# Shifted-window attention and a Fourier layer on one core: two groups transformed back in other rows, attention banks in strict turn, values fetched by ScalarE in three rows of eight, queries ahead of the late exponential

## The chip, the core and the metric

The kernel runs on one core of a Trainium2 chip. The metric is the device time of one execution in microseconds (us); the kernel before is measured in three runs and given by their median. All profile times come from one further, profiled execution.

A core has four engines that compute, and each works through its own queue in order: TensorE (PE; its weight loads are shown as PEld), ScalarE (ACT), VectorE (DVE) and GpSimd (POOL). SyncE (SP) issues most of the DMAs. [...]TensorE writes to PSUM, eight banks of 2 KB for each of 128 partitions.

## The reference, cut to what matters

Input: 32 images of 56x56 pixels and 128 channels, float32. Two layers, each added to its input:

```python
# layer 0: group norm (32 groups), then attention in shifted 7x7 windows, 4 heads of 32
x = x + attention(_gn(x), rpb_table, w_qkv, w_proj, b_proj)
#   q, k, v = win @ w_qkv.T;  softmax(q k^T * 32**-0.5 + bias + mask) v;  @ w_proj.T + b_proj
# layer 1: group norm, then a cosine transform along each axis, cut to 32 modes and mixed
h = _forward_fourier(_gn(x), w0, w1)
#   xy = idct(einsum('bixy,ioy->boxy', dct(x, axis=-1)[..., :32], w0)); xx: the same along the other axis
x = x + (relu(h @ W1 + b1) @ W2 + b2)
```

All of it is computed in float32.

## The kernel before, in words

**Rows.** The work is cut into rows: one row is 7 lines of one image, that is 8 windows. An image has 8 rows, and the 32 images have 256. The main loop counts cycles; in cycle r the products, scores and softmax of row r are made, the value product with the softmax belongs to row r-3, and so does the projection at the cycle's end. Below, "row 7" stands for a cycle whose number leaves 7 when divided by 8, "row 12" and greater numbers for single cycles. Cycles 0 to 10 (`first_rows`) carry attention alone. From cycle 11 on (`CONV_BEGIN`) each cycle also carries a share of the second layer of the image before: an image's own count `c` begins at 0 in its row 3 and goes to 15, so two images are in it at a time. After cycle 258 the second layer alone is left.

**Order.** The loop is inside `tc.manual_schedule` for TensorE, ScalarE, VectorE and GpSimd: on each of them instructions stand in the order in which the Python code emits them. SyncE's order is made by the scheduler of the Tile layer, which also sets every semaphore and gives buffers to tiles.

**A row's steps on the engines.**

- TensorE: q and k (`attn_qk`, L422, by `halved`, L113), ff_in (L113, from `xf`), the values (L549: softmax, turned, times v), a cosine transform (L705) in rows 3 to 5, the scores (L480), transforms back (`modes_back`, L792), the value product v (`attn_v`, L458), mixing of modes (`mix`, L753), ff_out (L113, from `hid`) and the projection (L594).
- ScalarE: copies of q (L435) and k (L445) out of PSUM, the squares for the second norm (`attn_squares`, L631), ReLU (`hid`, L837), half of the attention output (`oT`, L581), the copies of v (L465) and z (L761), the scaling of modes (L728), the exponential (`attn_exp`, L505), once an image the scaled weights `wn` (L414).
- VectorE: sums for the softmax (`sm`, L510) and its inverse, copies of projected rows (`x`, L602) and results (L880), the other half of oT in three instructions (L579: 147, 28 and 21 elements), the copies of the scores with bias (L488), their maximum (L498), transposes of modes (`turn_modes`, L721), adding the transform back to `xf` (`fetch_back`, L810), the transpose of the softmax (L534) and, in row 7, the chain of the first norm (`image_norm`, L382 to L411).
- GpSimd: subtracts the maximum (L499), divides by the sum (L524), adds biases (L127, L842), raises to the power -0.5 (L406).

**Banks.** Attention has four banks of PSUM under one tag (`pa`); the allocator gives a tile whichever bank its own model says comes free first. The second layer has the other four (`pc`). In `attn_values` the two banks are taken in reverse, so that half u = 0, which ScalarE reads, has the second one.

**Where things stand.** `halves_first`, `eighths`, `quarters`, `last_fetch`, `columns_turn`, `behind_max` and `halves_last` are emitted one after the other in each cycle (L1235 to L1260). The exponential of a row is emitted in `halves_last`, the copy of the next row's q in the next cycle's `halves_first`. `back_groups` (L922) says when the transforms back are made, four groups a direction (16, 16, 16 and 8 lines): at c = 5 and 6 along one axis, at c = 7 and 8 (rows 2 and 3) along the other. `load_back` issues their loads (zT) a cycle ahead. `FF_AT` (L42) places ff_in and ff_out at c = 8, 9, 10, 12, 13, 14, 15. `next_tokens` (L954) loads two rows ahead into the buffer `xr` which the squares used as scratch.

Of the kernel before, what the change touches and what calls it, by code (L numbers as in the profile page):

```python
# [1 line left out]

# [45 lines left out]
def swin_fourier_kernel(  # L48
# [32 lines left out]

    def attn_bank():
        return bank("pa", 4)
# [338 lines left out]
    def attn_qk(im, i):  # L422

        def product(part):
            p = attn_bank()
            w = im.w[:, part * C : (part + 1) * C]
            halved(p[:, :RT].rearrange("p (j t) -> p j t", t=WT), w, im.xw[i])
            if i == 0:
                halved(p[:, RT : RT + 1], w, im.mean)
            return p  # L430

        pq = product(0)
        if i == 0:
            nc.scalar.mul(im.bias[:, 0:1], pq[:, RT : RT + 1], QS)
        nc.scalar.activation(  # L435
            q_sb[:, :RT], pq[:, :RT], AF.Identity, bias=im.bias[:, 0:1], scale=QS
        )
        pk = product(1)
        if i == 0:
            for u in range(2):  # L440
                nc.scalar.mul(
                    im.bias[:, 3 + u : 4 + u], pk[:, RT : RT + 1], heads[:, u : u + 1]
                )
        for u in range(2):
            nc.scalar.activation(  # L445
                k_sb[:, u],
                pk[:, :RT].rearrange("p (w j) -> p w j", j=WT),
                AF.Identity,
                bias=im.bias[:, 3 + u : 4 + u],
                scale=heads[:, u : u + 1],  # L450
            )
# [85 lines left out]
    def attn_values(im, i, r):  # L537
# [3 lines left out]
        po = [attn_bank(), attn_bank()][::-1]  # L541
# [21 lines left out]
        for u in range(2):  # L563
            src = po[u][:, :HALF].rearrange("p (r f x) -> p r f x", r=WS, f=NP)
            n = NP - u
            dst = bass.AP(
                oTr.tensor,
                oTr[:, :, SS + u * WS :].offset,
                [oTr.ap[0], [S, WS], [2 * WS, n], [1, WS]],
            )  # L570
            parts = [(dst, src[:, :, :n])]
            if u:
                parts += [
                    (oTr[:, :, S - WS + SS :], src[:, :, n, : WS - SS]),
                    (oTr[:, :, 0:SS], src[:, :, n, WS - SS :]),
                ]
            for d, f in parts:
                if u:
                    nc.vector.tensor_scalar(d, f, im.bias[:, 2:3], None, ALU.add)  # L579
                else:  # L580
                    nc.scalar.activation(d, f, AF.Identity, bias=im.bias[:, 2:3])  # L581
# [44 lines left out]
    def attn_squares(im, i):  # L626

        n0, n1 = WS * i // 2, WS * (i + 1) // 2
        piece = x1[:, n0:n1]
        sq = im.xr.pop(i)[:, : n1 - n0]  # L630
        nc.scalar.activation(sq, piece, AF.Square, scale=valid)  # L631
        nc.vector.tensor_reduce(
            im.part[:, i % 4, 1],
            sq.rearrange("p n (g c) -> p g n c", c=4),
            axis=AX.XY,
            op=ALU.add,
        )
# [77 lines left out]
    def turn_modes(im, width, h):  # L715

        im.modes[width, h] = []
        for p in im.py.pop((width, h)):
            t = work.tile([P, 4, C], F32, tag="z", name="modes", bufs=4)
            t = t.rearrange("p k c -> p (k c)")[:, : 2 * CH * KB]  # L720
            nc.vector.transpose(t, p[:, : 2 * CH * KB])  # L721
            im.modes[width, h].append(t)
# [199 lines left out]
    def back_groups(c):  # L922

        if c in (5, 6, 7, 8):
            return [(c >= 7, (c + 1) % 2 * 2 + j) for j in range(2)]
        return []
# [37 lines left out]
    def halves_first(cycle):  # L964
# [4 lines left out]
        tokens_bias(cycle)  # L969
        if cycle == CONV_BEGIN or (cycle - 1) % NWR not in EARLY:  # L970
            divide(cycle)
# [3 lines left out]
        im, i = row(cycle)  # L975
        if im:
            attn_qk(im, i)
            if i == NWR - 2:
                wrap_rows(cycle)
        if last and cycle > CONV_BEGIN:  # L980
            attn_squares(last, j)
        next_tokens(cycle)
# [36 lines left out]
    def quarters(cycle):  # L1019
        def back():  # L1020
            for im, c in fourier(cycle):
                for j, (width, g) in enumerate(back_groups(c)):
                    modes_back(im, width, g)
                    if not (c == 8 and j):
                        fetch_back(im, width, g)
# [9 lines left out]
    def eighths(cycle):  # L1035
        im, i = row(cycle - 3)
        if im:
            attn_values(im, i, cycle - 3)
        for im, c in fourier(cycle):
            if c == 0:  # L1040
                for h in range(2):
                    transform(im, True, h)
                    turn_modes(im, True, h)
# [80 lines left out]
    EARLY = (0, 3, 4, 5, 7)  # L1124

    def halves_last(cycle):
# [11 lines left out]
        if row(cycle)[0]:  # L1138
# [18 lines left out]
    def first_rows(cycle):  # L1157
        im, i = row(cycle)
        im3, i3 = row(cycle - 3)
        if im:  # L1160
            attn_qk(im, i)
# [15 lines left out]
        if last:  # L1177
            attn_squares(last, j)
            add_sums(last, j)
# [27 lines left out]
        if cycle == CONV_BEGIN - 1:  # L1207
            attn_sums(im3, i3)
            attn_squares(im3, i3)
            attn_exp(cycle)  # L1210

    ET = mybir.EngineType
    with tc.manual_schedule(engines={ET.PE, ET.Activation, ET.DVE, ET.Pool}):
# [17 lines left out]
        for cycle in range(NB * NWR + CONV_BEGIN + FF_AT[-1] - NWR + 1):  # L1231
# [4 lines left out]
            if not row(cycle - 3)[0]:  # L1236
                eighths(cycle)
                columns_turn(cycle)
# [18 lines left out]
            columns_turn(cycle)  # L1257
# [65 lines left out]
```

## Time and profile before

| what | us |
|---|---|
| runs of the kernel before: median (lowest, highest) of 3 | 3269.87 (3268.61, 3271.36) |
| profiled execution, its own time | 3275.91 |
| its span, first to last instruction | 3274.1 |
| TensorE busy | 3147.8 |
| VectorE, GpSimd, ScalarE busy | 2637.3, 2340.5, 2099.2 |
| span of rows 24 to 247 (282.6 to 3036.9) | 2754.3 |
| one image in it, 28 of them | 98.4 |

How to read it. The page slices the span in 40 and gives the busy share of an engine in each slice as a digit; busy time of TensorE holds stretches in which its pipeline refills, so it is a bound and not a measure of its pace. The view of waits adds up, for each instruction group, the time that its engine stood idle right before it, and names what ended that: "PE pa L458 <- ACT oT L581: 15.6, 29, 1.0" reads that TensorE stood 15.6 us in all, in 29 places and at most 1.0 us at once, before products of L458 into a bank `pa`, until a ScalarE instruction of L581 was done. "issue" is idle time for which no wait is seen. The view of windows gives, for a stretch, its length and each engine's busy time in it. In the timeline a line has the start, the duration, the engine, the line of code and the operands; brackets give the idle time of the engine just before.

### The profile page before, as it was taken

The page shows a single profiled execution, that of the slowest core. Times are in us where ns is not written, and L with a number is a line of the kernel's source. Part 1 is how long each engine was busy: PE and PEld are TensorE (multiplying, and loading weights), DVE is VectorE, ACT ScalarE, POOL GpSimd, SP SyncE. Part 2 cuts the span into 40 slices and gives each one's busy share as a digit, 9 for nine tenths or more (in the row PEclk, how much of TensorE's full clock was granted, in tenths as well). Part 3 has the DMA queues.
Part 4 walks back from the last instruction along what each step waited for, and adds up shares of the span by engine and source line. Part 5 has one row for each costly group of instructions (what it writes and reads, how often), then busy time and mean ns, then how long its engine had stood idle before and what let it go on. Part 6 is the DMA issues. An engine that isn't in the chain of part 4 may idle for free.

```text
span 3274.1 us, 151714 instructions
## 1 busy us (share of the span) xinstructions
PE 3147.8 (96%) x65664; PEld 2369.2 (72%) x65664; DVE 2637.3 (81%) x5066; ACT 2099.2 (64%) x3680; POOL 2340.5 (71%) x2634
## 2 busy tenths in 40 slices
PE   4689999999999999999999999999999999999999
PEld 3467777777777777777777777777777777777776
DVE  7888888888888888888888888888888888888751
ACT  3456766666666666666666666666666666666663
POOL 7767777777777777777777777777777777777741
PEclk8789999999999999999999999999999999999999
DMA  6546555655565656565656665656565656565453
GB/s 111 111 115 148 139 135 142 140 137 144 137 146 141 143 140 145 134 143 139 144 137 145 142 139 136 146 136 143 138 145 138 146 136 143 137 144 138 121 138 99
DMA packets 1173442, 448.47 MB, mean 137 GB/s; under 512 B 529483, under 2 KB 1142909, under 8 KB 1172773
## 3 DMA queue, kind: packets, MB, share of 16 engines
q1 hardware_dynamic: 1163428, 433.22, 55.9%
q8 instruction: 516, 8.45, 1.2%
q10 hardware_dynamic: 8736, 5.38, 0.7%
q14 instruction: 154, 1.25, 0.1%
q0 software_dynamic: 608, 0.17, 0.0%
HBM read 277.00 MB, written 161.48 MB: 134 GB/s over the span
## 4 chain that ended last, share of the span: by engine, by line
PE 84%; ACT 7%; DVE 2%; issue 2%; DMA 2%; SPq 2%; POOL 1%; ACTq 0%; DVEq 0%; POOLq 0%
PE pc L113 38%; PE pa L113 10%; PE pa L458 8%; PE pc L792 5%; PE pa L594 5%; PE pa L480 5%; PE pc L753 5%; PE pa L549 4%; PE pc L705 3%; ACT hid L837 2%; ACT k L445 2%; SPq L763 1%; ACT xr L631 1%; ACT z L761 1%; DMA zscr<-z 1%
## 5 line engine op out<-in xcount | busy, mean ns | idle before, releaser
L524 POOL TENSOR_TENSOR blocks<-a,rs 128x512 f32<-128x512 f32 x1506 | 1278.9, 856 | 399.2 <-DVE rs L512 253.6
L113 PE MATMUL pc<-wff,hid 128*64 128x128 f32 x12288 | 715.3, 273 | 2.4 <-ACT hid L837 1.0
L113 PE MATMUL pc<-xf,wff 128*64 128x512 f32 (+2 forms) x3584 | 714.5, 539 | 1.1 <-DVE xf L810 0.9
L113 PEld LDWEIGHTS pc<-wff,hid 128*64 128x64 f32 x12288 | 679.6, 137 | 15.0 <-ACT hid L837 5.3
L499 POOL TENSOR_TENSOR a<-a,mx 128x784 f32<-128x784 f32 x251 | 377.4, 1504 | 351.0 <-DVE mx L498 334.3
L113 PEld LDWEIGHTS pc<-xf,wff 128*64 128x64 f32 x3584 | 267.1, 136 | 368.1 <-issue 254.5
L837 ACT ACTIVATE hid<-pc,b1sb 128x512 f32<-128x512 f32 (+2 forms) x896 | 500.0, 642 | 40.7 <-PE pc L113 40.7
L113 PE MATMUL pa<-xw,wn 128*64 128x392 f32 x2048 | 397.6, 503 | 30.2 <-ACT wn L414 29.7
L465 ACT COPY v<-pa 128x512 f32<-128x512 f32 x256 | 151.7, 593 | 419.8 <-PE pa L458 417.1
L488 DVE TENSOR_TENSOR a<-pa,bm 128x392 f32<-128x392 f32 x502 | 260.3, 560 | 90.4 <-PE pa L480 72.3
L445 ACT ACTIVATE k<-pa,bqkv,heads 128x392 f32<-128x392 f32 x512 | 318.6, 674 | 15.4 <-PE pa L113 1.3
L728 ACT ACTIVATE y<-modes,rstd 128x448 f32<-128x448 f32 x256 | 276.5, 1138 | 72.8 <-DVE modes L721 64.3
L842 POOL TENSOR_TENSOR res<-res,b2sb 128x512 f32<-128x512 f32 (+1 forms) x224 | 252.3, 1126 | 87.5 <-DMA res<-scr 87.5
L534 DVE STREAM_TRANSPOSE eT<-blocks 128x1024 f32<-128x1024 f32 x256 | 313.8, 1226 | 0.9 <-POOL blocks L524 0.9
L458 PE MATMUL pa<-wn,xw 128*64 128x128 f32 x4096 | 291.3, 284 | 22.5 <-ACT oT L581 15.6
L127 POOL TENSOR_TENSOR xr<-xr,bproj 128x384 f32<-128x384 f32 (+1 forms) x256 | 292.3, 1142 | 25.7 <-DMA xr<-in_x_dram 8.9
L505 ACT ACTIVATE a<-a 128x784 f32<-128x784 f32 x251 | 215.1, 857 | 147.3 <-POOL a L499 147.1
L549 PEld LDWEIGHTS pa<-eT,v 49*32 49x32 f32 x16384 | 173.6, 106 | 159.0 <-ACT hid L837 48.7
L435 ACT ACTIVATE q<-pa,bqkv 128x392 f32<-128x392 f32 x256 | 149.2, 583 | 210.4 <-PE pa L113 208.7
L579 DVE TENSOR_SCALAR oT<-pa,bqkv 128x147 f32<-128x147 f32 (+2 forms) x768 | 171.7, 280 | 135.9 <-PE pa L549 133.2
L510 DVE TENSOR_REDUCE sm<-a 128x16 f32<-128x784 f32 x251 | 241.4, 962 | 41.1 <-ACT a L505 40.9
L458 PEld LDWEIGHTS pa<-wn,xw 128*64 128x64 f32 x4096 | 227.6, 140 | 62.0 <-ACT oT L581 29.0
(112 smaller groups left out, 5040.0 us busy)
## 6 DMA issues: line engine op xcount, KB each, us to landing
zscr<-z SPq DMA_DIRECT2D x512, 112.0 KB
xin<-in_x_dram SPq DMA_DIRECT2D x496, 112.0 KB
htok<-scr SPq DMA_DIRECT2D x256, 196.0 KB
zT<-zscr SPq DMA_DIRECT2D x192, 256.0 KB
res<-scr SPq DMA_DIRECT2D x160, 256.0 KB
out_dram<-res SPq DMA_DIRECT2D x160, 256.0 KB
scr<-x SPq DMA_DIRECT2D x256, 112.0 KB
xr<-in_x_dram SPq DMA_DIRECT2D x256, 84.0 KB
```

Of the source, the lines that this page charges most:

```text
L113: nc.tensor.matmul(dst[ps], lhsT=lhsT[:, ps], rhs=rhs, start=start, stop=stop)
L127: nc.gpsimd.tensor_tensor(piece, piece, bproj.unsqueeze(1).to_broadcast([P, n, C]), ALU.add)
L445: nc.scalar.activation(k_sb[:, u], pk[:, :RT].rearrange("p (w j) -> p w j", j=WT), AF.Identity, bias=im.bias[:, 3 + u : 4 + u], scale=head ...
L458: nc.tensor.matmul(pv[HALVES[w % 2], w // 2 * C : (w // 2 + 1) * C], lhsT=im.half[i // NP][:, t0 : t0 + JP], rhs=im.w[:, 2 * C : 3 * C], s ...
L488: nc.vector.tensor_tensor(a[:, 2 * hp : 2 * hp + 2, :, 0:WT].rearrange("p u w j -> p w u j"), ps[hp][:, :RT].rearrange("p (w u j) -> p w u ...
L499: nc.gpsimd.tensor_tensor(a3, a3, mx.unsqueeze(2).to_broadcast([P, 2 * NWR, WT]), ALU.subtract)
L524: nc.gpsimd.tensor_tensor(dst[to, k, :, :n], a3[src, :, kb * KB : kb * KB + n], rs[src].unsqueeze(2).to_broadcast([src.stop - src.start, 2 ...
L534: nc.vector.transpose(eT.rearrange("p t (k j) -> p k t j", k=2), blocks[r % 2])
L549: nc.tensor.matmul(po4[u][h * HD : (h + 1) * HD, pr], lhsT=v[ks, pr, h * HD : (h + 1) * HD], rhs=eT[ks, h * NP + pr, :WT], start=True, sto ...
L728: nc.scalar.mul(y[:, r], t.rearrange("p (n k) -> p n k", k=NM), im.rstd)
L837: nc.scalar.activation(hf[:, :n], ph[:, :n], AF.Relu, bias=b1sb[:, f : f + 1])
L842: nc.gpsimd.tensor_tensor(im.res[:, :k], im.res[:, :k], b2sb.unsqueeze(1).to_broadcast([P, k, C]), ALU.add,)
```

## The change

- `attn_bank` gives the four attention banks in strict turn, each under a tag of its own with one buffer.
- `back_groups`: the two last groups of the second direction are made at c = 10 (16 lines, row 5) and c = 12 (8 lines, row 7) instead of both at c = 8 (row 3). Their products stay behind the scores; their copies (`fetch_back`) stand behind the maximum, in `last_fetch`. `turn_modes` is split by its two banks; where c = 10, the first bank is turned ahead of the scores' copy.
- In rows 3, 6 and 7 (`VALUES_BY_ACT`) ScalarE reads both halves of oT: u = 0 first, in one instruction, then u = 1 in three. The banks are then not reversed.
- `attn_qk` is split into `attn_q` and `attn_k`. In row 7 the exponential of the row before stands between them on ScalarE; it is no more emitted at the end of row 6.
- In row 7 the squares stand behind oT on ScalarE, their sum (`sum_squares`, VectorE) behind the maximum and the copies of the moved group, ahead of the norm's chain, and the load of tokens (`next_tokens`) behind that sum.

```diff
@@ -79,8 +80,10 @@
     def bank(tag, bufs):
         return psum.tile([P, HB], F32, tag=tag, name=tag, bufs=bufs)
 
+    turns = count()
+
     def attn_bank():
-        return bank("pa", 4)
+        return bank(f"pa{next(turns) % 4}", 1)
 
     def conv_bank():
         return bank("pc", 4)
@@ -419,23 +422,26 @@
         yield
 
 
-    def attn_qk(im, i):
-
-        def product(part):
-            p = attn_bank()
-            w = im.w[:, part * C : (part + 1) * C]
-            halved(p[:, :RT].rearrange("p (j t) -> p j t", t=WT), w, im.xw[i])
-            if i == 0:
-                halved(p[:, RT : RT + 1], w, im.mean)
-            return p
-
-        pq = product(0)
+    def product_of(im, i, part):
+        p = attn_bank()
+        w = im.w[:, part * C : (part + 1) * C]
+        halved(p[:, :RT].rearrange("p (j t) -> p j t", t=WT), w, im.xw[i])
+        if i == 0:
+            halved(p[:, RT : RT + 1], w, im.mean)
+        return p
+
+    def attn_q(im, i):
+
+        pq = product_of(im, i, 0)
         if i == 0:
             nc.scalar.mul(im.bias[:, 0:1], pq[:, RT : RT + 1], QS)
         nc.scalar.activation(
             q_sb[:, :RT], pq[:, :RT], AF.Identity, bias=im.bias[:, 0:1], scale=QS
         )
-        pk = product(1)
+
+    def attn_k(im, i):
+
+        pk = product_of(im, i, 1)
         if i == 0:
             for u in range(2):
                 nc.scalar.mul(
@@ -534,11 +540,13 @@
         nc.vector.transpose(eT.rearrange("p t (k j) -> p k t j", k=2), blocks[r % 2])
         im.eT[i] = eT
 
-    def attn_values(im, i, r):
+    def attn_values(im, i, r, both=False):
 
 
         v = v_sb[r % 3]
-        po = [attn_bank(), attn_bank()][::-1]
+        po = [attn_bank(), attn_bank()]
+        if not both:
+            po.reverse()
         HALF = RT // 2
         po4 = [p[:, :HALF].rearrange("p (r n s) -> p n r s", r=WS, s=WS) for p in po]
         eT = im.eT.pop(i)
@@ -560,7 +568,7 @@
 
 
         oTr = oT[:, i % 2 * RT : (i % 2 + 1) * RT].rearrange("p (r x) -> p r x", x=S)
-        for u in range(2):
+        for u in (0, 1) if both else (1, 0):
             src = po[u][:, :HALF].rearrange("p (r f x) -> p r f x", r=WS, f=NP)
             n = NP - u
             dst = bass.AP(
@@ -575,7 +583,7 @@
                     (oTr[:, :, 0:SS], src[:, :, n, WS - SS :]),
                 ]
             for d, f in parts:
-                if u:
+                if u and not both:
                     nc.vector.tensor_scalar(d, f, im.bias[:, 2:3], None, ALU.add)
                 else:
                     nc.scalar.activation(d, f, AF.Identity, bias=im.bias[:, 2:3])
@@ -627,11 +635,14 @@
 
         n0, n1 = WS * i // 2, WS * (i + 1) // 2
         piece = x1[:, n0:n1]
-        sq = im.xr.pop(i)[:, : n1 - n0]
-        nc.scalar.activation(sq, piece, AF.Square, scale=valid)
+        im.sq = im.xr.pop(i)[:, : n1 - n0]
+        nc.scalar.activation(im.sq, piece, AF.Square, scale=valid)
+
+    def sum_squares(im, i):
+
         nc.vector.tensor_reduce(
             im.part[:, i % 4, 1],
-            sq.rearrange("p n (g c) -> p g n c", c=4),
+            im.sq.rearrange("p n (g c) -> p g n c", c=4),
             axis=AX.XY,
             op=ALU.add,
         )
@@ -712,14 +723,13 @@
             at += n
         im.py[width, h] = py
 
-    def turn_modes(im, width, h):
-
-        im.modes[width, h] = []
-        for p in im.py.pop((width, h)):
-            t = work.tile([P, 4, C], F32, tag="z", name="modes", bufs=4)
-            t = t.rearrange("p k c -> p (k c)")[:, : 2 * CH * KB]
-            nc.vector.transpose(t, p[:, : 2 * CH * KB])
-            im.modes[width, h].append(t)
+    def turn_modes(im, width, h, r):
+
+        p = im.py[width, h][r]
+        t = work.tile([P, 4, C], F32, tag="z", name="modes", bufs=4)
+        t = t.rearrange("p k c -> p (k c)")[:, : 2 * CH * KB]
+        nc.vector.transpose(t, p[:, : 2 * CH * KB])
+        im.modes.setdefault((width, h), []).append(t)
 
     def scale_modes(im, width, h, r):
 
@@ -921,9 +931,9 @@
 
     def back_groups(c):
 
-        if c in (5, 6, 7, 8):
-            return [(c >= 7, (c + 1) % 2 * 2 + j) for j in range(2)]
-        return []
+        if c in (5, 6, 7):
+            return [(c == 7, (c + 1) % 2 * 2 + j) for j in range(2)]
+        return [(True, c // 2 - 3)] if c in (10, 12) else []
 
     def load_back(cycle):
         for im, c in fourier(cycle):
@@ -967,19 +977,27 @@
         if cycle % NWR == NWR - 1:
             norm_step(cycle)
         tokens_bias(cycle)
+        im, i = row(cycle)
+        behind_short = im and i == NWR - 1
+        if behind_short:
+            attn_q(im, i)
+            attn_exp(cycle - 1)
         if cycle == CONV_BEGIN or (cycle - 1) % NWR not in EARLY:
             divide(cycle)
         if last and cycle > CONV_BEGIN:
             attn_sums(last, j)
         next_quarter(cycle)
-        im, i = row(cycle)
         if im:
-            attn_qk(im, i)
+            if not behind_short:
+                attn_q(im, i)
+            attn_k(im, i)
             if i == NWR - 2:
                 wrap_rows(cycle)
-        if last and cycle > CONV_BEGIN:
+        if last and cycle > CONV_BEGIN and not behind_short:
             attn_squares(last, j)
-        next_tokens(cycle)
+            sum_squares(last, j)
+        if not behind_short:
+            next_tokens(cycle)
         if cycle % NWR == 0:
             norm_step(cycle)
         for im, c in fourier(cycle):
@@ -1019,9 +1037,9 @@
     def quarters(cycle):
         def back():
             for im, c in fourier(cycle):
-                for j, (width, g) in enumerate(back_groups(c)):
+                for width, g in back_groups(c):
                     modes_back(im, width, g)
-                    if not (c == 8 and j):
+                    if c < 8:
                         fetch_back(im, width, g)
 
         if not has_ff(cycle):
@@ -1035,12 +1053,15 @@
     def eighths(cycle):
         im, i = row(cycle - 3)
         if im:
-            attn_values(im, i, cycle - 3)
+            attn_values(im, i, cycle - 3, cycle % NWR in VALUES_BY_ACT)
+            if cycle % NWR == NWR - 1:
+                attn_squares(*row(cycle - 4))
         for im, c in fourier(cycle):
             if c == 0:
                 for h in range(2):
                     transform(im, True, h)
-                    turn_modes(im, True, h)
+                    for r in range(2):
+                        turn_modes(im, True, h, r)
                 next(im.stats)
             if c == 1:
                 for r in range(2):
@@ -1054,13 +1075,14 @@
 
     def last_fetch(cycle):
         for im, c in fourier(cycle):
-            if c == 8:
-                fetch_back(im, *back_groups(c)[1])
-
-    def columns_turn(cycle):
+            if c > 8:
+                for width, g in back_groups(c):
+                    fetch_back(im, width, g)
+
+    def columns_turn(cycle, r):
         for im, c in fourier(cycle):
             if c in (1, 2):
-                turn_modes(im, False, c - 1)
+                turn_modes(im, False, c - 1, r)
 
     def scale_first(cycle, r):
         for im, c in fourier(cycle):
@@ -1122,6 +1144,7 @@
                 ff_out(im, FF_AT.index(c))
 
     EARLY = (0, 3, 4, 5, 7)
+    VALUES_BY_ACT = (3, 6, 7)
 
     def halves_last(cycle):
         im, i = row(cycle)
@@ -1135,7 +1158,7 @@
         next_begin(cycle)
         if cycle % NWR == NWR - 1:
             norm_step(cycle)
-        if row(cycle)[0]:
+        if row(cycle)[0] and cycle % NWR != NWR - 2:
             attn_exp(cycle)
         scale_first(cycle, 1)
         if row(cycle)[0] and cycle % NWR in EARLY:
...
@@ -1250,11 +1277,19 @@
             if not has_ff(cycle):
                 half_columns(cycle)
             eighths(cycle)
+            early = any(c == 10 for _, c in fourier(cycle))
+            if early:
+                columns_turn(cycle, 0)
             quarters(cycle)
             if row(cycle)[0]:
                 attn_max(cycle)
+            if not early:
+                columns_turn(cycle, 0)
+            columns_turn(cycle, 1)
             last_fetch(cycle)
-            columns_turn(cycle)
+            if cycle % NWR == NWR - 1 and row(cycle - 4)[0]:
+                sum_squares(*row(cycle - 4))
+                next_tokens(cycle)
             behind_max(cycle)
             load_first(cycle)
             halves_last(cycle)
```

More of the change, by code (lines that the diff above doesn't have):

```diff
@@ L1 @@
 from contextlib import ExitStack
+from itertools import count
 import numpy as np
@@ L1160, in first_rows @@
         if im:
-            attn_qk(im, i)
+            attn_q(im, i)
+            attn_k(im, i)
         if cycle == NWR:
@@ L1178, in first_rows @@
             attn_squares(last, j)
+            sum_squares(last, j)
             add_sums(last, j)
@@ L1209, in first_rows @@
             attn_squares(im3, i3)
+            sum_squares(im3, i3)
             attn_exp(cycle)
@@ L1237, in swin_fourier_kernel @@
                 eighths(cycle)
-                columns_turn(cycle)
+                for r in range(2):
+                    columns_turn(cycle, r)
                 behind_max(cycle)
@@ L1255, in swin_fourier_kernel @@
                 attn_max(cycle)
+            if not early:
+                columns_turn(cycle, 0)
+            columns_turn(cycle, 1)
             last_fetch(cycle)
-            columns_turn(cycle)
+            if cycle % NWR == NWR - 1 and row(cycle - 4)[0]:
+                sum_squares(*row(cycle - 4))
+                next_tokens(cycle)
             behind_max(cycle)
```

## The prediction

> **What bounds the kernel now.** A row is one pass of the main loop (256 of them carry attention, eight per image); "row 7" is a row whose number leaves 7 divided by 8. I read the page first.
>
> ```profile
> span 3274.1 us, 151714 instructions
> PE 3147.8 (96%) x65664; PEld 2369.2 (72%) x65664; DVE 2637.3 (81%) x5066; ACT 2099.2 (64%) x3680; POOL 2340.5 (71%) x2634
> PE   4689999999999999999999999999999999999999
> PEclk8789999999999999999999999999999999999999
> ```
>
> TensorE (PE) is at 9 tenths or more from the fifth slice on: what doesn't shorten a wait of PE there is worth nothing. Next, the waits of PE alone, to see what such waits are.
>
> ```profile
> engine line waited for: us in total, times, longest us
> ...
> PE pa L458 <- ACT oT L581: 15.6, 29, 1.0
> PE pa L549 <- ACT q L435: 10.1, 4, 4.9
> PE pc L792 <- issue: 10.1, 12, 1.4
> ...
> PE pa L458 <- issue: 4.8, 9, 1.0
> ```
>
> 29 waits of the value product (L458) for ScalarE's read of the attention output (oT L581): about one per image, so a fixed place. The q waits are four and lie in the start. Then windows: the steady part, two instances of row 7.
>
> ```profile
> 282.60:3036.90 2754.30, 2721.28 (x57462) 2055.90 (x57460) 2300.24 (x4397) 1831.52 (x3220) 2033.25 (x2268) 1.00 0.59 141
> ```
> ```profile
> 1647.14:1661.02 13.88, 13.33 (x248) 9.78 (x246) 12.43 (x27) 8.84 (x15) 11.20 (x13) 1.00 0.59 168
> 2629.03:2642.29 13.26, 13.26 (x249) 9.78 (x247) 11.32 (x27) 8.85 (x15) 10.58 (x13) 1.00 0.62 177
> ```
>
> First number after the stretch is its length, the next PE's busy time. In 2754.3 us PE idles 33.0 us: a cap on any gain there. The two rows 7 have the same work; one idles 0.55 us and is 0.62 longer, the other idles nothing. What differs is in the timeline of the first:
>
> ```profile
> 1648.43 0.86 ACT L505 ACTIVATE a<-a 128x784 f32<-128x784 f32 x1 [1.36 <-POOL a L499]
> 1649.20 0.57 ACT L435 ACTIVATE q<-pa,bqkv 128x392 f32<-128x392 f32 x1
> 1649.67 1.24 ACT L445 ACTIVATE k<-pa,bqkv,heads 128x392 f32<-128x392 f32 x2
> 1650.79 0.72 ACT L631 ACTIVATE xr<-x,valid 128x512 f32<-128x512 f32 x1
> 1651.40 2.42 ACT L837 ACTIVATE hid<-pc,b1sb 128x512 f32<-128x512 f32 x4
> ...
> 1653.68 0.47 ACT L581 ACTIVATE oT<-pa,bqkv 128x196 f32<-128x196 f32 x1
> ...
> 1654.20 1.09 PE L458 MATMUL pa<-wn,xw 128*64 128x128 f32 x16 [0.55 <-ACT oT L581]
> ```
>
> ScalarE stands 1.36 us before the late exponential (L505), which waits for GpSimd's subtraction; q, k, the squares (L631), the four ReLUs (L837) and oT are queued behind it. oT ends 7.01 us into the row, and PE could have gone on at 6.44 (where the other row did; its exponential began 0.65 sooner).
>
> **What the Trainium skill says.** "PSUM — Partial Sum Buffer", section "Engine vs sequencer instructions": the queues of ScalarE, VectorE and GpSimd are strictly first in, first out. The trace agrees: q's product was there, and q's copy began 0.77 us after the exponential. "SBUF — State Buffer", section "SBUF: two separate sides": VectorE and GpSimd share a port pair by an exclusive lock, held for a whole instruction. It agrees: in this row L374 runs 1.31 us and ends at 1657.96, with GpSimd's L499 (1656.43 to 1657.93); elsewhere it takes 0.18. "ScalarE: Activation LUTs", section "Rules for kernel authors": about 0.3 us an activation and 0.83 ns an element; 196 elements give 0.46, the page of before has 456 ns.
>
> **The change, part by part** (offsets from the row's start).
>
> *Row 7 on ScalarE.* New order: q, exponential, k, ReLUs, oT, then the squares. q can start at 0.75 (its product's end), ends 1.33; the exponential still starts at GpSimd's end, 1.29 before, so about 1.35 to 2.2; k 2.2 to 3.4; the squares' 0.72 are gone from here. ReLUs: PE gives them every 0.9 us, the last at 4.93; they run 3.4 to 5.9. The first oT half, 0.46, ends at 6.35. PE wants the value product after the scores (6.44) and now after the moved group (0.46 more, below): 6.9. Margin 0.55, and the order of the changed program gives the value product the bank of that first half. The three more oT instructions (147, 28, 21 elements): by the skill's price 0.42 + 0.32 + 0.32 = 1.06, an estimate; bounds 0.67 (VectorE's L579 for all three) and 1.37 (three times the 196-element row). I take 1.0; it runs 6.35 to 7.35, the squares to 8.05, and the value copy, ready at 7.85, is that late: the z copies come at 8.7, nobody waits. Hidden at both bounds. Gain: the list's 15.6 us less the 1.0 of row 15, which ends in a 5.2 us wait for the next image's weights anyway: 14.6, times 0.62/0.55 for the refill: **-16.4 us**.
>
> *The same oT in rows 3 and 6.* +1.0 on ScalarE, -0.67 on VectorE each; the value copy there starts after 4.24 and 1.19 us of ScalarE's idle time: 0. Row 6's own wait (0.06) stays: first half and order unchanged.
>
> *Two groups moved.* L792 on idctw: 48 matmuls, 1.44 us, leave row 3; 32 (0.96) go to row 5, 16 (0.48) to row 7. Sum 0. Their copies (L810, VectorE) go along: 1.14 and 0.68. In row 5 PE's last product needs a bank of the transform: that transpose (L721, first half) goes ahead of the scores' copy, 0.58 us where VectorE idled 1.07. In row 7 ff_out takes the first L810's bank: scores 6.54, copies and maximum to 8.6, L810 at 9.0, PE there at 9.6. Hidden by 0.6; past that each 0.1 costs 3 us. The xf lines are read in rows 7 and 1, two rows on. zT loads are moved past other SP issues, no new one; both buffers are then held longer, and the next image's second zT load stands on SP till row 7's group is done (7.4), needed only 13 us later.
>
> *Sum of squares behind the maximum, token load behind it.* Row 7: VectorE's norm chain (L389 to L402) starts 1.37 us later (0.68 + 0.69), but L374's 0.7 behind L499 goes: wn, ended 12.63 of 13.88, ends about 13.3 at most 14.0, against 13.72 now. I take 13.3: 0, range up to 0.3 an image (9 us). The xr load is issued at 10 instead of 5.1, on SP ahead of z stores ready then; it is needed 10 us later, and elsewhere 7.5 suffice (row 130 to 131). Behind the waiting SP stands nothing due: 0.
>
> *Banks in strict turn.* In steady rows each bank's last reader is old either way: 0. In rows 0, 1, 2, 4, 5 the value product now follows VectorE's oT, done 0.9 to 1.6 us ahead. In the start it matters: rows 12 and 17 before wait for q (PE resumes at 142.59 and 199.61), in strict turn for L602 of the row before, which ends at 143.8 and 202.7. Row 12: +1.2, of which VectorE's queue (oT at 146.4) hides 0.5; row 17: +3.1, of which the zT wait to 202.43 hides most, 1.05 is left. Row 12's nearest cover may hide all, or row 13 double it: 0 to 4; I take **+1.8**.
>
> *Instruction issue.* Idle "issue" of PE on L792, L458 and near is 16.8 us in this span (waits list: 10.1, 4.8 and two of 1). It comes where small matmuls are thick: values, transform, scores, L792. Row 3 loses the mix (4.8 of the 16.8), rows 5 and 7 get it. From -6 to +7; I take **+1**.
>
> Sum: -16.4 + 1.8 + 1.0 = -13.6. The profiled execution took 3275.91 (span 3274.1 and 1.8 around it): 3262.3 by the sum. The runs' median is 6.0 below it; taking the same off it, 3269.9 - 13.6 = **3256.3 us**, 0.42% less.
>
> **Rivals.** (a) *The norm chain becomes the start of the next image's row.* For it: 1.37 us put ahead of a slack of 1.24; against: L374's port wait falls. Should that wait find another GpSimd instruction instead, wn ends at 12.63 + 1.37 + 0.7 = 14.7 against 13.72: 1.0 us in 31 images, +31 - 13.6: 3287. It turns the sign from 0.44 us past the row's end on. Chance 0.08. (b) *The gain is eaten*: thick rows 5 and 7 cost +7, the start +4: -16.4 + 11 = -5.4: 3264.5, no change. The start's waits are plain in the trace, the issue's size isn't: 0.17. (c) *More*: row 3's issue waits go and none come, start even: -16.4 - 6: 3247.5. Chance 0.12. (d) That it doesn't do what it says, the wait staying: needs oT 0.55 later than worked out; ReLUs are set by PE's pace: 0.03, 3272. My forecast: 0.60, own range 3250 to 3262.
>
> **Numbers.** About 0.2% (6.5 us) is what a measurement here can tell from no change. Faster: 0.60 + 0.12 + 0.05 of (b) = 0.77. Same: 0.12 of (b) and 0.03 = 0.15. Slower 0.08. The range 3246 to 3266 takes in (b) and nearly all of (c), and leaves (a) and (d) out.
>
> **What would show it.** Right: the list's L458 on oT falls from 15.6 to under 2; row 7 lasts 13.7 with the moved group, row 3 1.4 less. Wrong: a wait of L113 on wn in each image (a), more issue waits on rows 5 and 7 (b), L549 on x L602 above 4 us in the start. If L810 in row 7 is late, a wait of ff_out on xf appears.

## The result and the profile after

| | runs, us: median (lowest to highest) | profiled execution, own time | its span |
|---|---|---|---|
| before, beside it | 3270.61 (3268.61 to 3274.52), 4 runs | 3275.91 | 3274.1 |
| changed | 3246.11 (3244.34 to 3251.14), 4 runs | 3245.75 | 3244.0 |

The ratio is 0.9929, 95% interval 0.9917 to 0.9942: 24.5 us less, where 13.6 were forecast. The 3246.11 lie 0.1 us above the lower end of the forecast's range (3246 to 3266) and outside its own narrower one (3250 to 3262). Executions in a slow state are left out of all ratios; the profiled one of experiment 6 below was one (3647.66 us, at a granted clock of 0.85), so that kernel has no row lengths. The two profiled executions lie 30.2 us apart, because that of before was 5.3 us above its median; the traces below are to be read against the 30.

The page of the changed kernel, for the lines shown of before:

```profile
span 3244.0 us, 151708 instructions
PE 3136.1 (97%) x65664; PEld 2363.2 (73%) x65664; DVE 2538.4 (78%) x4787; ACT 2165.5 (67%) x3959; POOL 2343.1 (72%) x2634
PE   5689999999999999999999999999999999999999
PEclk8789999999999999999999999999999999999999
```

TensorE has the same 65664 matmuls and is busy 11.7 us less: so not all of the gain was idle time. Its waits, in the list of the changed kernel:

```profile
PE pa L116 <- ACT wn L417: 29.8, 2, 24.1
PE pa L602 <- DVE oT L587: 20.5, 7, 6.3
PE pa L557 <- DVE x L610: 15.8, 5, 5.6
PE pc L802 <- issue: 8.1, 12, 1.6
...
PE pa L464 <- issue: 3.3, 7, 0.7
```

The 15.6 us of the value product (now L464) on ScalarE's oT are gone; a wait of the values (L557) for the copy of the row before (x L610) has come, and that for q has gone. Windows of the changed kernel: the steady part (rows 24 to 247), then one row 3, row 5 and row 7. Behind the length stand the busy times of PE, PEld, DVE, ACT and POOL with their instructions in brackets, then the granted clock, the share of DMA and GB/s.

```profile
280.76:3006.39 2725.63, 2710.70 (x57460) 2050.26 (x57458) 2209.12 (x4145) 1891.73 (x3473) 2035.36 (x2269) 1.00 0.60 142
806.20:819.50 13.30, 13.30 (x256) 9.09 (x254) 9.84 (x19) 9.59 (x17) 10.63 (x14) 1.00 0.58 142
832.17:845.42 13.25, 13.25 (x280) 9.40 (x278) 11.79 (x22) 9.22 (x15) 9.14 (x10) 1.00 0.69 134
853.86:867.50 13.64, 13.64 (x265) 10.13 (x263) 10.85 (x25) 9.25 (x18) 10.53 (x12) 1.00 0.53 156
```

The steady part fell from 2754.30 to 2725.63: 28.7 of the 30 us are there, 1.02 in each of 28 images. The same three rows of the kernel before:

```profile
812.49:827.34 14.85, 14.85 (x305) 10.38 (x303) 12.74 (x27) 9.11 (x14) 11.21 (x14) 1.00 0.54 129
840.00:852.46 12.46, 12.46 (x248) 8.67 (x246) 10.42 (x19) 8.47 (x14) 8.94 (x10) 1.00 0.73 144
860.90:874.77 13.87, 13.32 (x249) 9.77 (x246) 12.40 (x27) 8.84 (x15) 11.19 (x13) 1.00 0.58 161
```

Row 7 is 0.23 shorter although it has 16 matmuls more. Row 5 rose by 0.79 where 0.96 were forecast; row 3 fell by 1.55 where 1.44 were. In row 3 of before TensorE is "busy" for the whole 14.85 us. The gain that was not forecast therefore came out of busy time: in the steady part it fell by 10.6 us (2721.28 to 2710.70), and idle time by 18.1 (33.0 to 14.9).

The new row 7 on ScalarE, in the timeline of the changed kernel (row start 853.86):

```profile
854.80 0.59 ACT L438 ACTIVATE q<-pa,bqkv 128x392 f32<-128x392 f32 x1 [1.01 <-PE pa L116]
855.29 0.85 ACT L511 ACTIVATE a<-a 128x784 f32<-128x784 f32 x1
856.03 1.24 ACT L451 ACTIVATE k<-pa,bqkv,heads 128x392 f32<-128x392 f32 x2
857.16 2.43 ACT L847 ACTIVATE hid<-pc,b1sb 128x512 f32<-128x512 f32 x4
859.55 1.05 ACT L589 ACTIVATE oT<-pa,bqkv 128x196 f32<-128x196 f32 x4
860.47 0.74 ACT L639 ACTIVATE xr<-x,valid 128x512 f32<-128x512 f32 x1
```

It is the forecast's chain: oT starts at 5.69 (859.55 - 853.86) where 5.9 was worked out, and the value product at 6.82 with no wait.

### The profile page after: what moved, and what is told of

It reads as the page before. It is cut to its first block, busy times and chain, and to the rows that moved or that the text cites. A ratio compares the mean times of both kernels' runs of the same rounds, so it can differ in the third digit from the quotient of the medians.

```text
span 3244.0 us, 151708 instructions
## 1 busy us (share of the span) xinstructions
PE 3136.1 (97%) x65664; PEld 2363.2 (73%) x65664; DVE 2538.4 (78%) x4787; ACT 2165.5 (67%) x3959; POOL 2343.1 (72%) x2634
## 5 line engine op out<-in xcount | busy, mean ns | idle before, releaser
L505 POOL TENSOR_TENSOR a<-a,mx 128x784 f32<-128x784 f32 x251 | 377.7, 1505 | 285.6 <-DVE mx L504 270.2
L464 PE MATMUL pa<-wn,xw 128*64 128x128 f32 x4096 | 291.2, 284 | 7.1 <-issue 3.3
L557 PEld LDWEIGHTS pa<-eT,v 49*32 49x32 f32 x16384 | 173.1, 106 | 161.1 <-issue 63.9
L602 PE MATMUL pa<-wproj,oT 128*64 128x128 f32 x3584 | 246.4, 276 | 20.7 <-DVE oT L587 20.5
L464 PEld LDWEIGHTS pa<-wn,xw 128*64 128x64 f32 x4096 | 227.5, 140 | 45.5 <-ACT oT L589 8.1
```

The lines of the kernel that those rows point to most:

```text
L464: nc.tensor.matmul(pv[HALVES[w % 2], w // 2 * C : (w // 2 + 1) * C], lhsT=im.half[i // NP][:, t0 : t0 + JP], rhs=im.w[:, 2 * C : 3 * C], s ...
L505: nc.gpsimd.tensor_tensor(a3, a3, mx.unsqueeze(2).to_broadcast([P, 2 * NWR, WT]), ALU.subtract)
L602: nc.tensor.matmul(pp[hs, (n - n0) * C : (n - n0 + 1) * C], lhsT=oT[:, t0 : t0 + JP], rhs=wproj, start=True, stop=True,)
```

## The experiments

Theory A: the old place of the groups held waits for banks in row 3, which ended when VectorE had emptied them and which TensorE's idle time doesn't show; leaving that place is the gain that was not forecast. Its rivals: the prices of the forecast with a gain from elsewhere (B: strict turn, oT on ScalarE, fewer issue waits), and a supply of instructions that 48 small matmuls in one stretch outrun (C).

Row lengths are medians over rows 24 to 247 in the trace, from the first product of q to that of the next row; "image" is the mean over 28 images. Ratios are to the kernel before on the same chip, with 95% interval.

| kernel | row 3 | row 5 | row 6 | row 7 | image | ratio |
|---|---|---|---|---|---|---|
| before | 14.87 | 12.45 | 8.43 | 13.88 | 98.37 | 1 |
| changed | 13.30 | 13.22 | 8.44 | 13.64 | 97.34 | 0.9929 (0.9917 to 0.9942) |
| 1 row 7's order alone | 14.86 | 12.45 | 8.43 | 13.26 | 97.59 | 0.9946 (0.9934 to 0.9959) |
| 2 groups alone | 13.30 | 13.22 | 8.43 | 13.64 | 97.14 | 0.9919 (0.9905 to 0.9932) |
| 3 changed, groups in row 3 | 14.86 | 12.45 | 8.43 | 13.26 | 97.47 | 0.9943 (0.9931 to 0.9956) |
| 4 changed, one group in row 3 | 14.07 | 12.45 | 8.44 | 13.64 | 97.32 | 0.9937 (0.9923 to 0.9950) |
| 5 before, copy into xf first | 14.64 | 12.45 | 8.43 | 13.88 | 98.29 | 0.9986 (0.9980 to 0.9993) |
| 6 before, transpose twice | | | | | | 1.0054 (1.0040 to 1.0068) |
| 7 changed, no strict turn | 13.30 | 13.21 | 8.43 | 13.64 | 97.35 | 0.9923 (0.9910 to 0.9937) |
| 8 changed, start on ScalarE | 13.30 | 13.21 | 8.43 | 13.64 | 97.47 | 0.9929 (0.9917 to 0.9942) |
| 9 changed, oT as before | 13.30 | 13.22 | 8.38 | 13.67 | 97.31 | 0.9909 (0.9895 to 0.9922) |
| 10 groups, z later in row 6 | 13.30 | 13.22 | 8.29 | 13.79 | 97.20 | 0.9910 (0.9896 to 0.9923) |
| 11 changed, again | 13.30 | 13.22 | 8.44 | 13.64 | 97.63 | 0.9937 (0.9923 to 0.9950) |
| 12 groups, row 7's order, z later | 13.30 | 13.22 | 8.30 | 13.64 | 97.28 | 0.9909 (0.9895 to 0.9923) |

**1. Row 7's order alone.** `attn_q`, `attn_k`, the late exponential and the squares of the change (with their sum and the token load), nothing else. The part of the edit that sets the order:

```diff
+        if behind_short:
+            attn_q(im, i)
+            attn_exp(cycle - 1)
...
-        if row(cycle)[0]:
+        if row(cycle)[0] and cycle % NWR != NWR - 2:
             attn_exp(cycle)
```

> The kernel before with row 7's new order on ScalarE and VectorE alone (q, late exponential, k, ReLUs, oT, squares); banks, oT's engines and groups as before. Both theories: row 7 falls from 13.88 to 13.26 us (the stall goes, no group is there), the other rows keep their lengths, so 31 x 0.62 = 19 us less, about 3252; the forecast's own price was 16.4. If it gains 24 us, this part makes the whole change and nothing is left for the groups.

Measured: 3252.87 against 3271.38, 18.5 us less (13 to 22 by the interval). Row 7 is at 13.26, its length without a stall. The first term of the forecast has its size; some of the gain is left to explain.

**2. The groups alone.** Only `back_groups`, `last_fetch` and `columns_turn` as changed.

```diff
-        if c in (5, 6, 7, 8):
-            return [(c >= 7, (c + 1) % 2 * 2 + j) for j in range(2)]
-        return []
+        if c in (5, 6, 7):
+            return [(c == 7, (c + 1) % 2 * 2 + j) for j in range(2)]
+        return [(True, c // 2 - 3)] if c in (10, 12) else []
```

> The kernel before with the two groups moved to rows 5 and 7 and nothing else. Theory A (the old place held two bank waits in row 3 that the idle time of TensorE doesn't show): row 3 falls from 14.87 to 13.3-13.4, row 5 rises by 0.77 to 13.22, row 7 stays at 13.88, because the 16 matmuls fill the stall: 31 x 0.74 = 23 us less, about 3248. Theory B (the forecast's prices: 30 ns a matmul wherever it stands): row 3 -1.44, row 5 +0.96, row 7 0, so 15 us less, about 3256.

Measured: 3243.46, 27.9 us less, as much as the whole change. Rows 3 and 5 are as theory A has them; row 7 was expected to stall still (13.88) and doesn't. Its timeline (row start 850.36), ScalarE and then TensorE:

```profile
851.40 0.86 ACT L505 ACTIVATE a<-a 128x784 f32<-128x784 f32 x1 [1.11 <-POOL a L499]
...
856.64 0.48 ACT L581 ACTIVATE oT<-pa,bqkv 128x196 f32<-128x196 f32 x1
```
```profile
856.69 0.56 PE L791 MATMUL pc<-idctw,zT 64*64 64x112 f32 x16
857.18 1.10 PE L458 MATMUL pa<-wn,xw 128*64 128x128 f32 x16
```

The queue on ScalarE is the old one, but the late exponential starts 1.04 into the row (1.29 in the row of before shown in the prediction; why, was not followed up), so oT ends at 6.76; and the 16 matmuls that came into the row put the value product off from 6.44 to 6.82. Two small shifts, 0.25 and 0.38, cover the stall of 0.55, with 0.06 to spare. Row 7's new order on ScalarE is a second cure of what the groups cure already: 18.5 and 27.9 don't add up.

**3. The changed kernel with both groups back in row 3.**

```diff
-            return [(c == 7, (c + 1) % 2 * 2 + j) for j in range(2)]
-        return [(True, c // 2 - 3)] if c in (10, 12) else []
+            return [(c >= 7, (c + 1) % 2 * 2 + j) for j in range(2)]
+        return []
```

(with 8 among the values of `c` again, and `fetch_back` in its old places).

> The changed kernel with both groups back in row 3, all else as changed. Theory A: rows 3, 5 and 7 last 14.87, 12.45 and 13.26, together 0.42 more than in the changed kernel, so 31 x 0.42 = 13 us more than it, about 3259; ff_out in row 3 begins 3.25 us after the scores as before. Rival (the gain beyond the stall comes from the banks' strict turn, from oT on ScalarE or from fewer issue waits): the same as the changed kernel, 3246, or within 3 us.

Measured: 3251.24, 5.1 above the changed kernel's median, between the two expectations; by the intervals the time can't be told from the changed kernel's, so the row lengths decide. They are those of theory A to 0.01 us; the mean image is only 0.13 longer than the changed one's, because less idle time on "issue" fell into this execution (7.6 us in rows 24 to 247 against 12.8). By the intervals it can't be told from experiment 1 either: banks and oT on ScalarE bring nothing that shows.

**4. One group in row 3.** In the changed kernel the 16 lines go to row 3 instead of row 5.

```diff
-        return [(True, c // 2 - 3)] if c in (10, 12) else []
+        return [(True, c // 4)] if c in (8, 12) else []
```

(and `fetch_back` right behind its products).

> The changed kernel with the group of 16 lines (32 matmuls) in row 3 instead of row 5; the 8 lines stay in row 7. Theory A: ff_out in row 3 takes the bank that VectorE's first L820 frees only 3.2 us after the scores began, however few matmuls stand ahead of it: row 3 lasts 14.7-14.9 (1.5 more), row 5 0.77 less, so 31 x 0.7 = 22 us more than the changed kernel, about 3268. Rival (48 small matmuls in one stretch outrun the supply of instructions, 32 don't): 3246 to 3248.

Measured: 3249.36; row 3 lasts 14.07, 0.77 more than without the group: theory A's number missed by far, and the rival's lies within the interval (3246 to 3255). The timeline of row 3 shows why A's number was wrong, TensorE and then VectorE:

```profile
812.70 0.94 PE L802 MATMUL pc<-idctw,zT 64*64 64x112 f32 x32
813.58 1.09 PE L464 MATMUL pa<-wn,xw 128*64 128x128 f32 x16
814.50 0.94 PE L116 MATMUL pc<-wff,hid 128*64 128x128 f32 x14
```
```profile
813.62 1.02 DVE L494 TENSOR_TENSOR a<-pa,bm 128x392 f32<-128x392 f32 x2
814.57 1.14 DVE L820 TENSOR_TENSOR xf<-pc,xf 128x448 f32<-128x448 f32 x2
```

ff_out starts before VectorE's copy (L820) does. One group fills two of the four banks `pc`, and the program gives ff_out one of the two others; both groups fill all four, and ff_out must take one that the copy frees. That is a reading after the fact, so two kernels were made to decide between A and the supply of instructions.

**5. The copy first.** The kernel before, row 3 only: VectorE copies the first group into `xf` ahead of the scores.

```diff
+        late = any(c == 8 for _, c in fourier(cycle))
+        if im and not late:
+            scores_copy(*s)
         if has_ff(cycle):
             back()
+        if im and late:
+            scores_copy(*s)
```

> The kernel before; in row 3 VectorE copies the first transformed group into xf ahead of the scores instead of behind them (the maximum ends at the same time). Theory A (ff_out in row 3 waits about 0.17 us for the bank which that copy frees, unseen in the idle time of TensorE): the value product is followed by ff_out after 0.92 us instead of 1.10, row 3 lasts 14.68 instead of 14.86, 31 x 0.17 = 5 us less, 3265. Theory C (48 small matmuls in one stretch outrun the supply of instructions): row 3 as before, 3270.

Measured: 4.3 us less (2.3 to 6.6 by the interval) with not one matmul moved; row 3 lasts 14.64. Row 3 of before, TensorE, its weight loads and VectorE:

```profile
820.61 1.51 PE L792 MATMUL pc<-idctw,zT 64*64 64x112 f32 x48
822.05 1.09 PE L458 MATMUL pa<-wn,xw 128*64 128x128 f32 x16
823.14 0.33 PE L113 MATMUL pc<-wff,hid 128*64 128x128 f32 x2
```
```profile
823.13 0.20 PEld L113 LDWEIGHTS pc<-wff,hid 128*64 128x64 f32 x4 [0.23 <-DVE xf L810]
```
```profile
819.22 2.24 DVE L721 STREAM_TRANSPOSE modes<-pc 128x448 f32<-128x448 f32 x4
821.39 0.22 DVE L668 SCALAR_TENSOR_TENSOR nm<-ms 128x1 f32<-128x1 f32 x1
821.53 1.02 DVE L488 TENSOR_TENSOR a<-pa,bm 128x392 f32<-128x392 f32 x2
822.47 1.14 DVE L810 TENSOR_TENSOR xf<-pc,xf 128x448 f32<-128x448 f32 x2
```

and of experiment 5:

```profile
822.22 1.09 PE L458 MATMUL pa<-wn,xw 128*64 128x128 f32 x16
823.15 0.50 PE L113 MATMUL pc<-wff,hid 128*64 128x128 f32 x6
```

From value product to ff_out it is 1.09 before (822.05 to 823.14) and 0.93 with the copy first. The wait stands in brackets on the weight load (PEld), not on the matmul: the matmuls ahead last 0.27 us each in the records and overlap, so TensorE counts as busy over the gap. The view of one line's instructions, for L810 of before, has it as a sum:

```profile
who waited for it (us, times):
  PEld pc L113: 7.2, 25
  PE pc L113: 0.9, 3
```

25 waits, 0.29 us each: 16 of them in rows 3 of the steady part (3.9 us), the rest behind row 247. With the copy first, the 8 that are left all lie behind row 247:

```profile
who waited for it (us, times):
...
  PEld pc L113: 3.0, 8
```

Of the 28 rows 3 in the steady part, 18 have 1.05 us or more from value product to ff_out before, and 26 have 0.93 or less with the copy first. The forecast read the waits of PE alone.

**6. The first transpose twice.** The kernel before; in row 3 VectorE does the first of four transposes of modes (L721) two times.

```diff
-            nc.vector.transpose(t, p[:, : 2 * CH * KB])
+            for _ in range(2 if width and h == 0 and not im.modes[width, h] else 1):
+                nc.vector.transpose(t, p[:, : 2 * CH * KB])
```

> The kernel before; in row 3 VectorE does the first of the four transposes of modes twice (0.56 us more on its queue). Theory A (row 3 goes at VectorE's pace, through banks): the transforms back take about 2.0 us instead of 1.44, row 3 lasts 15.4 instead of 14.86, 31 x 0.56 = 17 us more, 3288. Theory C (supply of instructions to TensorE): 1.44 us and 14.86 as before, 3270.

Measured: 0.54% more (0.40 to 0.68), that is 17.7 us, or 0.57 for each of 31 images: 0.56 us on VectorE come out whole. Row 3 of before goes at VectorE's pace, though TensorE is busy throughout; the supply of instructions as the cause falls.

**7. No strict turn.**

```diff
-        return bank(f"pa{next(turns) % 4}", 1)
+        return bank("pa", 4)
```

> The changed kernel with the four attention banks given by the allocator again. If the forecast's prices hold, rows 12 to 18 wait for q again and not for the copy of the row before, which gives 1.8 us back: 3244; the steady rows keep their lengths. Rival (the strict turn is what saves time in the steady rows): 3250 or more.

Measured: 0.9923 against 0.9929: the same. The steady rows don't change; row 19 begins at 218.46 against 218.56, row 24 at 281.2 against 280.8. The waits for x are gone from the list and those for q are back (11.5 us, 4 times).

**8. The start on ScalarE.**

```diff
-            attn_values(im, i, cycle - 3, cycle % NWR in VALUES_BY_ACT)
+            attn_values(im, i, cycle - 3, cycle < 19 or cycle % NWR in VALUES_BY_ACT)
```

(and the same in `first_rows`).

> The changed kernel with ScalarE reading both halves of oT in all rows up to 18 as well, since VectorE is what TensorE waits for there (20.5 us before the projection on oT, 15.8 before the values on x). VectorE has 0.67 us less in each of these rows: row 19 begins 4 to 8 us sooner, 3238 to 3242. If ScalarE's queue (exponential, q, k) is late instead, nothing or a loss of up to 5 us.

Measured: 0.9929, no gain. Row 8 begins at 87.6 instead of 91.3, but lasts 18.8 instead of 15.4; row 9 is back at 106.4 (106.6). TensorE then waits 8.96 us in front of row 9 for VectorE's copy of scores: the start has another bound behind this one.

**9. oT as before.** `VALUES_BY_ACT = ()` in the changed kernel.

> The changed kernel with half of oT on VectorE again in all rows (no rows with both halves on ScalarE), all else as changed. The forecast gave this part 0 in rows 3 and 6 and hid it in row 7: rows keep their lengths, 3246. Rival (in row 7 VectorE's first copy of the moved group then comes 0.67 us later than with the part, past the 0.6 us in hand, and ff_out waits): row 7 longer by about 0.1, 3 us more, 3249.

**11. The changed kernel again**, on the chip of experiments 9 and 10.

> The changed kernel once more, beside the two others of this call: 3246, ratio 0.993. If the groups alone are the better kernel, they stand at 0.992 and this one at 0.993, not told apart.

Measured: 3247.83 for 9 and 3256.40 for 11, before 3278.66. Rows 3, 5 and 7 are the same to 0.03; row 6 is 0.05 longer with the part. So in the row lengths it is worth about 0, as forecast. But 8.6 us lie between the two, and the intervals of their ratios don't meet: on this chip the kernel without the part was faster. The two traced executions are 6.1 us apart (3250.27 and 3256.40), and 5.7 of that is idle time on "issue" in rows 24 to 247: 12.6 us in 9, 18.3 in 11. In the first trace of the same changed kernel it was 12.8. Whether the part has a share in it is not shown.

**10. z later in row 6.** The groups alone; in row 6 ScalarE's second copy of z stands behind oT.

> The kernel before with the two groups moved, as in the second experiment, and in row 6 ScalarE's second copy of z behind its half of oT, so that oT is not queued behind both copies. The value product in row 6 then starts 0.97 us after the scores began less 0.13: row 6 lasts 8.30 instead of 8.43, 31 x 0.13 = 4 us less than the groups alone (3243.5): 3239. If oT is bound by the values' end and not by the queue, row 6 stays at 8.43: 3243.

**12. The same with row 7's new order** (the changed kernel without the strict turn and without `VALUES_BY_ACT`).

> The changed kernel without the banks' strict turn and without oT on ScalarE (row 7's new order and the moved groups remain), and in row 6 the second copy of z behind oT. If row 7's new order is what keeps row 7 at 13.64 when row 6 is 0.14 shorter (with the groups alone row 7 gave the 0.14 back), rows 6 and 7 last 8.29 and 13.64: 31 x 0.14 = 4 us less than the changed kernel's rows, ratio 0.990 to before. If the 0.14 is given back elsewhere (the next row's start), the ratio is 0.991 as with the groups alone.

The edit of both (in `mix` the second copy is held back, and made behind `eighths`):

```diff
             eighths(cycle)
+            for im, c in fourier(cycle):
+                if short and c == 3:
+                    mixed(im, *im.held)
```

Measured: row 6 falls to 8.3 in both. In 10 row 7 gives it back (13.79): the value product waits 0.08 us for oT again, since the late exponential now comes 1.20 into the row instead of 1.04. In 12 row 7 stays at 13.64. The ratios are 0.9910 and 0.9909, so 4 us of rows are below what these runs tell apart. Both lie under the changed kernel's two measurements (0.9929 and 0.9937), clearly so only against the second. They are the fastest found, level with experiment 9.

## Why the forecast was right, and where it was wrong

The direction was right, and so was the size of the stall that was to carry the gain; the total was not. That 3246.11 still lies in the forecast's range is luck, by 0.1 us. The lower end was there for rival (c), 3247.5, whose cause (row 3's waits on "issue" go and none come) is not what the runs show. What failed is the premise at the head of the prediction: that what doesn't shorten a wait of TensorE is worth nothing, and that its 33.0 us of idle time are all there is to gain. (The page has TensorE at 9 tenths from the fourth slice on, not the fifth.) The steady part fell by 28.7 us, and 10.6 of them came out of busy time.

- **Row 7's stall, -16.4: right in size, wrong in what it adds.** The mean of row 7 stood 0.57 above its shortest in before and 0.00 in the changed kernel: 15.9 us in the 28 images of the steady part; alone, this part gave 18.5. But the moved group cures the same stall by itself, and beside it the new order adds nothing that shows (ratio 0.9919 without it, 0.9929 with it and the rest of the change). The forecast had both numbers in hand: with the group ahead of it the value product is due at 6.9, and oT's old order is done at 7.01, which leaves 0.11 of the 0.55. It held 6.9 only against the new order.
- **The two groups, "Sum 0": wrong, the term that was mis-sized.** Shortest lengths of rows 3, 5 and 7: 14.81, 12.45, 13.26 before and 13.30, 13.21, 13.64 after: -1.51 + 0.76 + 0.38 = -0.37 an image, -10.4 in 28. The forecast took 1.44 us for 48 matmuls in row 3, 30 ns each, and carried that price to rows 5 and 7. But there they add 24 ns each (0.76 for 32, 0.38 for 16), and in row 1, not moved, 48 take 1.26. The 1.44 held 0.18 us of waiting, and ff_out behind it waited 0.17 more. Experiment 5 takes the second wait away and experiment 6 shows the row tied to VectorE. That the 0.18 are the wait for the bank of the fourth transpose is argued only from its end (8.97 us into the row) and the break in the matmuls there (8.98); no run takes it away alone.
- **oT on ScalarE, 0: right** in the row lengths (9), open in the times, where the kernel without it was faster by 8.6 us; four instructions took 1.05 where 1.46 was allowed (0.46 and 1.0).
- **Norm chain, 0: right.** In the changed row 7 `wn` ended at 13.18 (forecast 13.3), 0.46 ahead of the row's end. The step on the port lock (the Trainium skill, "SBUF — State Buffer", section "SBUF: two separate sides") held in part. VectorE, then GpSimd:

```profile
863.55 1.01 DVE L392 TENSOR_TENSOR turned<-turned,gmeans 128x32 f32<-128x32 f32 x1
...
865.04 0.18 DVE L377 TENSOR_SCALAR gmeans<-gsums 128x32 f32<-128x32 f32 x1
```
```profile
863.01 1.50 POOL L505 TENSOR_TENSOR a<-a,mx 128x784 f32<-128x784 f32 x1
```

L377, the old L374, took 0.18 us (in before only 4 of its 64 instances did; most took 0.6 or 1.3). But L392, in before 0.18 as L389, took 1.01, begun beside GpSimd's L505 (9.15 to 10.65) and ended with it. The wait moved along the chain, which rival (a) had as its danger; it was shorter than before, 0.83 for 1.13 by these figures.

- **Strict turn, +1.8: not shown.** The exchange of waits came: those for q went and those on x came, 5.60 us in row 12 and 4.71 in row 17. But row 19 begins at 218.56 with the strict turn and at 218.46 without it (experiment 7), so no price shows. Against before (217.05) it is 1.5 us later, but the kernel of experiment 5, which differs from before only from row 19 on, has it at 219.96: the start scatters by more than the term. The forecast named waits on x "above 4" as a sign that it was wrong; the sign came and cost nothing that shows.
- **Instruction issue, +1: can't be told in the sum, but the place moved as it said.** Idle time on "issue" in rows 24 to 247 was 16.8 us in before, 12.8 and 18.3 in two executions of the changed kernel; this scatter is larger than the term. In before 4.9 of it lay in rows 3 and 0.9 in rows 5, after 1.6 and 4.4, and none in rows 7: what left row 3 came back in row 5, against rival (c).

What "issue" is, the traces can say. In before it has 26 places in rows 24 to 247. Each of them is the instruction 193 or 194 behind a multiple of 256 in TensorE's own list (matmuls, weight loads and its few semaphore instructions), and each wait ended 1.3 to 1.7 us after a packet of 16 KB had landed on the queue for instructions:

```profile
q8 instruction: 516, 8.45, 1.2%
```

That is one packet for every 256 of TensorE's 132215 instructions. At the 426 other such places of the steady part, without a wait, the median from landing to start is 4.5 us. So this idle time is a wait for the next block of instructions. In all the other traces it stands at the same place of 256, 193 to 195. In before it falls to L792 (12 times), L458 (9), L753 (3) and L113 (2), so into the small matmuls or right behind them; a group that moves takes its share along.

In the steady part the two terms give -15.9 - 10.4 = -26.3; with the 4.0 less of issue that is 1.6 more than the 28.7 measured. Open stays why the blocks come late more often in one execution than in another of the same kernel, and whether that is all of the difference between experiments 9 and 11.

## What to carry to other kernels

Read the waits of the weight loads beside those of the matmuls: a wait of 0.2 us behind overlapping matmuls doesn't appear as idle time of TensorE, and a row that is "busy" throughout can still go at another engine's pace, so idle time is no cap on what a change can gain. Take the price of a step that is to be moved from a place where nothing holds it up; a high price in the old place is itself the gain. And where two parts of a change push the same stall, measure each alone before adding them.

## What the hardware showed that was not expected

- 48 matmuls of 64x112 took 1.26 us in row 1 and 1.44 in row 3, with TensorE busy in both.
- TensorE's idle time on "issue" in rows 24 to 247 ranged from 7.6 to 18.3 us over the kernels here, all with 65664 matmuls, and differed by 5.5 us between two executions of one kernel. Every such wait stood at one place in 256 of TensorE's instructions, shortly after a 16 KB packet of instructions had landed.
